# A graph attention layer: one head's mask added by VectorE, the residual in other buffers, and a new instruction scheduler

## The chip, the cores and the metric

The kernel runs on one core of one Trainium2 chip. The metric is the device time of one execution in microseconds (us); the median of several executions is quoted. All runs here were in the normal ("fast") state. A ratio is the recorded ratio of one kernel's fast runs to the kernel before's fast runs of the same rounds on the same chip. It is not quite the ratio of the medians quoted, nor that of the plain means (up to 0.2 points off; a point is 1% of the kernel before's time). Ratios are what is compared across rounds. The rounds of the experiments ran on five chips, and an interval covers its own rounds alone.

Engine names in the profile: PE is TensorE, PEld its weight load, DVE VectorE, ACT ScalarE, POOL GpSimd (which in both kernels' profiles issues the accumulating transfers alone, 428 and 368 of them, on the software queue) and SP the engine that issues all plain transfers and transposes there. SPq is SP's queue.

## The reference, cut to what matters

For 32 graphs of 512 nodes with 512 features: layer norm and relu, a graph attention layer with 4 heads of 256, elu, a second one with one head of 512, and a residual.

```
def gat_layer(x, mask, W, a_src, a_dst, bias, concat):
    xl = (x @ W).reshape(B, N, H, F)
    e = leaky_relu(asrc[:, :, None, :] + adst[:, None, :, :], 0.2)
    e = where(mask[..., None], e, -1e9)
    attn = softmax(e, axis=1)
    out = einsum('bsdh,bshf->bdhf', attn, xl)
    ...
mask = (adj > 0) | eye(N)          # adj of the inputs is symmetric
h = elu(gat_layer(h, mask, W1, ..., b1, concat=True))
x + gat_layer(h, mask, W2, ..., b2, concat=False)
```

## The kernel before

The program first records every operation as a job (engine, assumed cost, what it reads and writes); a list scheduler then orders each engine's queue, and only that order is emitted. The waits come from the data, so an order can be slow but not wrong. A job's `cost` and `size` are the scheduler's beliefs and reach the chip only through the order.

The products are done in seven block products instead of eight (Strassen's scheme), so VectorE forms sums of blocks before and after each product. All graphs are pipelined: while one graph's second layer runs, the next one's first layer and the one after's projection run beside it.

The mask `m` (0 or a large negative number, bf16, one buffer for all graphs) is built by VectorE. It is stored to DRAM as `md` (in the profile: dm) and transposed by a transfer into `mt`:

```
def masks(b):
    ...                                        # m[:, t, :] from adj; m = max(m, diag)
    if b < B - 1:
        MASK[b] = mk, md = mds.take()
        dma(512e3, every, [mk], md..., m...)
    tk, mt = mts.take()
    prog.add("SP", 2.2, every, [tk],
        lambda: nc.sync.dma_start_transpose(mt..., m...), 300e3)
```

`first(h)` makes the row scores of a head with `mt`; `second(h)` makes the attention itself, p, and adds the mask either on VectorE from `m` or by two transfers that accumulate `md` into p:

```
here = self.b == B - 1 or self.layer == 1 and (h in HERE or self.b == 0 and h < H - 1)
for u in range(NT):
    dve(..., scalar_tensor_tensor, p[:, u, :], ...)
    if here:
        dve(..., nc.vector.tensor_add, p[:, u, :], p[:, u, :], m[:, u, :])
if not here:
    for us in (0, 1), (2, 3):
        accumulate(500e3, keys + [mk], keys, p..., md...)     # a GpSimd transfer with accum_op=add
```

The residual, x plus the second bias, waits in four buffers until the last products are added to it:

```
def residual(b, places=(xrs,) * NT):
    for d in range(NT):
        xk, xr = places[d].take()
        dma(256e3, (), halves, xr, x[b, d * P : (d + 1) * P, :])
        if places[0] is xrs:
            accumulate(256e3, [xk], halves, xr, rows_of(b2, P))
        else:
            dve(..., nc.vector.tensor_add, xr, xr, b2_sb)
```

The elu uses the same `xrs` (xr) buffers. The first gather, `sums1`, uses `ts_` (t), also four, for its sums of p. One round of the main loop:

```
gather1(s, 0); s.second(2); s.second(3)          # s: first layer of graph i+1
S2[i] = second_layer(i); S2[i].second(0)         # second layer of graph i
masks(i + 2); project1(i + 2) ...; n.first(0) ...  # front of graph i+2
gather1(s, 1)
residual(i); gather2(i, ...)
load(i + 3); project2(i + 1, ...)
```

## Time and profile before

| | kernel before |
|---|---|
| time, median (range) | 2859.48 us (2850.74 to 2864.9) |
| span in the profile | 2856.2 us |
| TensorE busy / idle | 2774.1 / 82.1 us |
| VectorE busy | 2584.4 us (90%) |
| accumulating transfers: mask into p, bias into xr | 304 and 124 |
| software queue: bytes, share of the time of the 16 transfer engines | 191.92 MB, 30.3% |

Idle time of an engine is span less busy time. TensorE bounds the kernel; what it waits for is in the prediction. Two views also belong here. The page's list of transfers gives the size and the median time from issue to landing for those of GpSimd:

```profile
p<-dm POOLq DMA_DIRECT2D x304, 512.0 KB, 5.1
...
xr<-in_L_gnn_b_dram POOLq DMA_DIRECT2D x124, 256.0 KB, 5.8
```

And the view of the mask tile m, for the transpose (count, then least, median and greatest duration of the issue in ns). SP issued nothing else meanwhile in the stretches shown here:

```profile
L463 SPq DMA_TRANSPOSE mt<-m x32: 1572/1923/4054, 32.2 to 2697.4; - x32
```

In the timeline around one of these transposes, the neighbours on GpSimd's queue are 14 us before it and 9 us behind it. SP goes on 0.05 us after its end:

```profile
1557.41 0.86 POOL L327 DMA_DIRECT2D p<-dm  x1 [2.94 <-PE mm L333]
1580.67 0.86 POOL L327 DMA_DIRECT2D p<-dm  x1 [22.40 <-DVE p L319]
```
```profile
1571.34 1.58 SPq L463 DMA_TRANSPOSE mt<-m  x1
1572.97 1.30 SPq L322 DMA_DIRECT2D rr<-drr  x1
```

### The profile page before, as it was taken

The page shows a single profiled execution, that of the slowest core. Times are in us where ns is not written, and L with a number is a line of the kernel's source. Part 1 is how long each engine was busy: PE and PEld are TensorE (multiplying, and loading weights), DVE is VectorE, ACT ScalarE, POOL GpSimd, SP SyncE. Part 2 cuts the span into 40 slices and gives each one's busy share as a digit, 9 for nine tenths or more (in the row PEclk, how much of TensorE's full clock was granted, in tenths as well). Part 3 has the DMA queues.
Part 4 walks back from the last instruction along what each step waited for, and adds up shares of the span by engine and source line. Part 5 has one row for each costly group of instructions (what it writes and reads, how often), then busy time and mean ns, then how long its engine had stood idle before and what let it go on. Part 6 is the DMA issues. An engine that isn't in the chain of part 4 may idle for free. (4 is left out here: it accounts for less than half of the span.)

```text
span 2856.2 us, 41534 instructions
## 1 busy us (share of the span) xinstructions
PE 2774.1 (97%) x12456; PEld 2365.5 (83%) x12456; DVE 2584.4 (90%) x6567; ACT 2306.4 (81%) x4861; POOL 416.7 (15%) x466
## 2 busy tenths in 40 slices
PE   7999999999999999999999999999999999999997
PEld 6668888888888888888888888888888888888875
DVE  7979998989999989899898999999998999999995
ACT  6878798888888888887888888888888888888872
POOL 0011111111111111111111111111111111111100
PEclk9999999999999999999999999999999999999999
DMA  6577777687786777776777877778767778777724
GB/s 204 150 174 182 188 203 188 180 193 194 181 210 181 194 185 191 201 191 182 189 188 182 207 176 183 202 190 206 190 179 194 189 187 215 176 192 191 182 68 128
DMA packets 389455, 527.23 MB, mean 185 GB/s; under 512 B 227184, under 2 KB 231280, under 8 KB 389232
## 3 DMA queue, kind: packets, MB, share of 16 engines
q1 hardware_dynamic: 327600, 332.68, 41.7%
q0 software_dynamic: 61632, 191.92, 30.3%
q8 instruction: 99, 1.62, 0.2%
q14 instruction: 124, 1.02, 0.1%
HBM read 344.72 MB, written 50.79 MB: 138 GB/s over the span
## 5 line engine op out<-in xcount | busy, mean ns | idle before, releaser
L333 PE MATMUL mm<-w_sb,hs 128*128 128x257 f32 (+1 forms) x3024 | 693.2, 383 | 19.4 <-ACT xl L316 10.8
L333 PEld LDWEIGHTS mm<-w_sb,hs 128*128 128x128 f32 x3024 | 574.0, 191 | 113.6 <-ACT xl L316 20.0
L327 POOL DMA_DIRECT2D p<-dm x304 | 267.5, 882 | 2032.1 <-DVE p L319 1034.3
L316 ACT ACTIVATE l<-as,z 128x512 f32<-128x512 f32 x640 | 441.8, 723 | 113.6 <-DMA as<-das 101.7
L316 ACT ACTIVATE l<-l,low 128x512 f32<-128x512 f32 x640 | 459.5, 723 | 71.5 <-DVE low L319 69.0
L316 ACT ACTIVATE p<-p,z 128x512 f32<-128x512 f32 x640 | 432.8, 722 | 103.4 <-DMA p<-dm 75.2
L333 PE MATMUL mm<-p,xl 128*128 128x256 f32 (+1 forms) x2016 | 489.5, 391 | 6.4 <-ACT p L316 3.5
L319 DVE SCALAR_TENSOR_TENSOR p<-rr,z 128x512 f32<-128x512 f32 x640 | 457.8, 745 | 37.2 <-DMA rr<-drr 36.8
L333 PE MATMUL mm<-w_sb,ht 128*128 128x258 f32 x2112 | 481.5, 382 | 2.2 <-ACT xl L316 1.2
L333 PE MATMUL mm<-w_sb,h 128*128 128x257 f32 x2056 | 470.0, 380 | 6.2 <-DVE h L319 4.3
L319 DVE CUSTOM_DVE_ANT_1 l<-l,mt 128x512 f32<-128x512 f32 x640 | 427.4, 683 | 46.2 <-ACT l L316 44.8
L333 PEld LDWEIGHTS mm<-w_sb,ht 128*128 128x128 f32 x2112 | 400.5, 190 | 64.1 <-ACT xl L316 4.0
L333 PEld LDWEIGHTS mm<-p,xl 128*128 128x128 f32 x2016 | 382.9, 190 | 82.6 <-issue 19.4
L333 PEld LDWEIGHTS mm<-w_sb,h 128*128 128x128 f32 x2056 | 389.9, 190 | 65.7 <-DVE h L319 5.3
L316 ACT ACTIVATE xl<-mm 128x258 f32<-128x258 f32 (+2 forms) x752 | 281.7, 384 | 49.0 <-PE mm L333 46.5
L319 DVE TENSOR_TENSOR xl<-xl,mm 128x258 f32<-128x258 f32 x558 | 224.8, 417 | 36.6 <-PE mm L333 28.7
L316 ACT ACTIVATE h<-mm 128x256 f32<-128x256 f32 x480 | 175.4, 379 | 84.2 <-PE mm L333 82.0
L316 ACT ACTIVATE xr<-h,b_sb 128x512 f32<-128x512 f32 x240 | 171.5, 723 | 77.3 <-DVE h L319 76.8
L333 PE MATMUL mm<-t,hs 128*128 128x256 f32 x960 | 218.3, 380 | 1.2 <-ACT h L316 0.9
L333 PEld LDWEIGHTS mm<-t,hs 128*128 128x128 f32 x960 | 183.1, 191 | 27.0 <-ACT h L316 1.3
L319 DVE TENSOR_TENSOR xr<-mm,xr 128x256 f32<-128x256 f32 (+1 forms) x424 | 170.9, 417 | 28.4 <-PE mm L333 19.9
L319 DVE SCALAR_TENSOR_TENSOR h<-h,b_sb,xr 128x512 f32<-128x512 f32 x240 | 175.9, 745 | 20.0 <-ACT xr L316 19.2
(105 smaller groups left out, 3427.6 us busy)
## 6 DMA issues: line engine op xcount, KB each, us to landing
p<-dm POOLq DMA_DIRECT2D x304, 512.0 KB, 5.1
rr<-drr SPq DMA_DIRECT2D x160, 512.0 KB
x<-in_x_dram SPq DMA_DIRECT2D x129, 256.0 KB
adj<-in_adj_dram SPq DMA_DIRECT2D x128, 256.0 KB
as<-das SPq DMA_DIRECT2D x64, 512.0 KB
xr<-in_x_dram SPq DMA_DIRECT2D x124, 256.0 KB
xr<-in_L_gnn_b_dram POOLq DMA_DIRECT2D x124, 256.0 KB, 5.8
out_dram<-xr SPq DMA_DIRECT2D x124, 256.0 KB
```

Source lines behind the costliest of these rows:

```text
L316: prog.add("ACT", cost, reads, writes, lambda: nc.scalar.activation(*a, **k))
L319: prog.add("DVE", cost, reads, writes, lambda: f(*a, **k))
L327: lambda: nc.gpsimd.dma_start(to, at, accum_op=OP.add), 1.4 * size,
L333: f(*a, **k)
```

## The change

Three parts. (H) The fourth head's mask in the first layer is added by VectorE, which takes 60 accumulating transfers away. (T) The residual moves from the xr to the t buffers, so that it can be loaded before the elu is done. (S) The scheduler gets costs closer to measured ones, decides transfers no earlier than 3.5 us ahead, and runs 40 more passes that raise the rank of what stood in the chain before a gap of TensorE. The diff, cut to its core (most changed costs are left out):

```
-    CROSS, SAME = 0.15, 0.1
-    DMA_LEAD, DMA_TAIL, DMA_RATE = 1.2, 1.0, 280e3
+    CROSS, SAME = 0.15, 0.07
+    PAIRS = {("PE", "ACT"): 0.21, ("PE", "DVE"): 0.21, ("DVE", "POOL"): 0.58, ("POOL", "DVE"): 0.4}
+    DMA_LEAD, DMA_TAIL, AHEAD = 0.8, 2.0, 3.5
...
+    def sooner(self, rank, start, cause):
+        jobs, lost, free = self.jobs, {}, 0.0
+        for j in range(len(jobs)):
+            if jobs[j][0] != "PE":
+                continue
+            gap, free = start[j] - free, start[j] + jobs[j][1]
+            d = cause[j]
+            while gap > 0.05 and d is not None and start[j] - start[d] < self.SPAN:
+                lost[d] = max(lost.get(d, 0.0), gap)
+                d = cause[d]
+        return [r - self.GAIN * lost.get(j, 0.0) for j, r in enumerate(rank)]
...
+            if e in ("SP", "POOL"):
+                t = max(t, hold)
...
+        for _ in range(self.REPAIRS):
+            rank = self.sooner(rank, start, cause)
+            start, cause = look(rank)
...
-    HERE = ()
+    HERE = (3,)
...
-            here = self.b == B - 1 or self.layer == 1 and (h in HERE or self.b == 0 and h < H - 1)
+            here = self.b == B - 1 or self.layer == 1 and (h in HERE if self.b else h < H - 1)
...
-                        500e3, keys + [mk], keys,
+                        2.2, keys + [mk], keys,
...
-    def residual(b, places=(xrs,) * NT):
+    def residual(b, places=(ts_,) * NT):
...
-            if places[0] is xrs:
-                accumulate(256e3, [xk], halves, xr, rows_of(b2, P))
+            if places[0] is ts_:
+                accumulate(1.56, [xk], halves, xr, rows_of(b2, P))
```

More of the change, by code (lines that the diff above doesn't have):

```diff
@@ L78, in latency @@
         if self.jobs[a][0] != self.jobs[b][0]:
-            return self.CROSS
+            return self.PAIRS.get((self.jobs[a][0], self.jobs[b][0]), self.CROSS)
         return 0.0 if self.jobs[a][0] == "PE" else self.SAME
@@ L85, in forwards @@
         n = len(jobs)
+        cause = [None] * n
         left = [len(job[2]) for job in jobs]
@@ L94, in forwards @@
         while len(done) < n:
-            j, t = self.next_job(rank, free, soon, ready, tensor, left, ready_at)
+            j, t = self.next_job(rank, free, soon, ready, tensor, left, ready_at, landed - self.AHEAD)
             start[j] = t
@@ L99, in forwards @@
             if jobs[j][4] is not None:
-                landed = max(landed, t + jobs[j][1] + self.DMA_LEAD) + jobs[j][4] / self.DMA_RATE
+                landed = max(landed, t + jobs[j][1] + self.DMA_LEAD) + jobs[j][4]
             for s in after[j]:
@@ L105, in forwards @@
                     r = t + jobs[j][1] + self.latency(j, s)
-                ready_at[s] = max(ready_at[s], r)
+                if r > ready_at[s]:
+                    ready_at[s], cause[s] = r, j
                 left[s] -= 1
@@ L109, in forwards @@
                     heappush(soon[jobs[s][0]], (ready_at[s], s))
-        return start, done
+        return start, done, cause
+    def sooner(self, rank, start, cause):
[9 more added lines that the diff above has]
+        return [r - self.GAIN * lost.get(j, 0.0) for j, r in enumerate(rank)]
+    SPAN, GAIN = 60.0, 2.0
     def backwards(self, rank):
@@ L124, in backwards @@
                 if jobs[j][4] is not None:
-                    moving = max(moving, ready_at[j]) + jobs[j][4] / self.DMA_RATE
+                    moving = max(moving, ready_at[j]) + jobs[j][4]
                     ready_at[j] = moving + self.DMA_LEAD
@@ L141, in backwards, with next_job @@
                     found.append(d)
-    def next_job(self, rank, free, soon, ready, tensor, left, ready_at):
+    def next_job(self, rank, free, soon, ready, tensor, left, ready_at, hold=0.0):
         best = None
@@ L178, in order @@
         for j in reversed(range(n)):
-            later = self.DMA_LEAD + self.DMA_TAIL + (jobs[j][4] or 0.0) / self.DMA_RATE
+            later = self.DMA_LEAD + self.DMA_TAIL + (jobs[j][4] or 0.0)
             need[j] = max(
@@ L190, in order, with look @@
                 pe = j
-        rank, best, self.tried = need, None, []
-        for _ in range(self.ROUNDS):
-            back = self.backwards(rank)
-            late = [-back[j] - jobs[j][1] for j in range(n)]
-            start, done = self.forwards(late)
+        best, self.tried = None, []
+        def look(rank):
+            nonlocal best
+            start, done, cause = self.forwards(rank)
             end = max(start[j] + jobs[j][1] for j in range(n))
@@ L198, in order @@
             if best is None or end < best[0]:
-                best = end, start, done, late
-            rank = [-start[j] - jobs[j][1] for j in range(n)]
-        _, self.start, done, self.late = best
+                best = end, start, done, cause, rank
+            return start, cause
+        rank = need
+        for _ in range(self.ROUNDS):
+            back = self.backwards(rank)
+            rank = [-back[j] - jobs[j][1] for j in range(n)]
+            start, cause = look(rank)
+            rank = [-start[j] - jobs[j][1] for j in range(n)]
+        _, start, _, cause, rank = best
+        for _ in range(self.REPAIRS):
+            rank = self.sooner(rank, start, cause)
+            start, cause = look(rank)
+        _, self.start, done, _, self.late = best
         return done
+    REPAIRS = 40
     def emit(self):
@@ L326, in accumulate @@
             "POOL", cost, reads, writes,
-            lambda: nc.gpsimd.dma_start(to, at, accum_op=OP.add), 1.4 * size,
+            lambda: nc.gpsimd.dma_start(to, at, accum_op=OP.add), size,
         )
@@ L360, in weights1 @@
                     dma(
-                        256e3, (), [("w1", ix, k)], w1_sb[:, ix, k, :, 2:],
+                        0.75, (), [("w1", ix, k)], w1_sb[:, ix, k, :, 2:],
                         w1[row : row + P, :].rearrange("p (j c f) -> p c j f", j=H // 2, c=2)[:, c],
@@ L370, in scores1 @@
                 dma(
-                    256e3, (), [vk + ("v", a, j)], bc[:, 2 * a + j, :],
+                    0.75, (), [vk + ("v", a, j)], bc[:, 2 * a + j, :],
                     bass.AP(tensor=v.tensor, offset=v.offset + j * 2 * FH, ap=[[0, P], [1, 2 * FH]]),
@@ L397, in weights2 @@
             dma(
-                512e3, [("ht", 0, 0)], [("w2", ix)], w2_sb[:, ix, :, 1 - c : W2H - c],
+                1.5, [("ht", 0, 0)], [("w2", ix)], w2_sb[:, ix, :, 1 - c : W2H - c],
                 w2[r * HF // 2 : (r + 1) * HF // 2, c * DO // 2 : (c + 1) * DO // 2].rearrange(
@@ L402, in weights2 @@
             )
-        dma(4e3, (), ["b1"], b1_sb[:, 0], b1.rearrange("(c p) -> p c", p=P))
+        dma(0.1, (), ["b1"], b1_sb[:, 0], b1.rearrange("(c p) -> p c", p=P))
         dve(TINY, ["b1"], ["b1"], nc.vector.tensor_scalar_mul, b1_sb[:, 1], b1_sb[:, 0], -1.0)
-        dma(256e3, (), ["b2"], b2_sb, rows_of(b2, P))
+        dma(0.75, (), ["b2"], b2_sb, rows_of(b2, P))
         for a, v in enumerate((as2, ad2)):
             lk, bc = ls.take()
-            dma(256e3, (), [lk], bc, rows_of(v[0], P))
+            dma(0.75, (), [lk], bc, rows_of(v[0], P))
             for (r, c), ix in AT.items():
@@ L437, in load @@
             xk, xt = xs.take()
-            dma(256e3, (), [xk], xt, x[b, t * P : (t + 1) * P, :])
+            dma(0.75, (), [xk], xt, x[b, t * P : (t + 1) * P, :])
             XT[b].append((xk, xt))
@@ L444, in masks @@
             ak, a = adjs.take()
-            dma(256e3, (), [ak], a, adj[b, t * P : (t + 1) * P, :])
+            dma(0.75, (), [ak], a, adj[b, t * P : (t + 1) * P, :])
             dve(
@@ L458, in masks @@
             MASK[b] = mk, md = mds.take()
-            dma(512e3, every, [mk], md.rearrange("p t n -> p (t n)"), m.rearrange("p t n -> p (t n)"))
+            dma(0.45, every, [mk], md.rearrange("p t n -> p (t n)"), m.rearrange("p t n -> p (t n)"))
         tk, mt = mts.take()
@@ L465, in masks @@
             ),
-            300e3,
+            2.5,
         )
@@ L494, in norm_turn @@
         act(
-            0.62, [xk, sk + (t,)], [xk], hn, hn, AF.Relu,
+            0.71, [xk, sk + (t,)], [xk], hn, hn, AF.Relu,
             bias=st[:, t, S : S + 1], scale=st[:, t, S + A : S + A + 1],
@@ L514, in norm_turn @@
             act(
-                1.14, [xk], [ak], words.rearrange("p (h f) -> p h f", h=2),
+                0.96, [xk], [ak], words.rearrange("p (h f) -> p h f", h=2),
                 hn.bitcast(U16).rearrange("p (f h) -> p h f", h=2), AF.Copy,
@@ L523, in norm_turn @@
                 ),
-                200e3,
+                1.27,
             )
             act(
-                1.14, [xk], [("ht", t, 0), ("ht", t, 1)],
+                1.21, [xk], [("ht", t, 0), ("ht", t, 1)],
                 ht[:, :, t * P : (t + 1) * P].bitcast(U16).rearrange("p k (n h) -> p h k n", h=2),
@@ L563, in spread @@
             dma(
-                0, [ok], [dk], dr[:k].rearrange("k (b j) -> b k j", j=32),
+                0.03, [ok], [dk], dr[:k].rearrange("k (b j) -> b k j", j=32),
                 bass.AP(
@@ L570, in spread @@
             dma(
-                256e3 * rows, [dk], [ok], o[:, :rows].rearrange("p r n -> p (r n)"),
+                0.72 * rows, [dk], [ok], o[:, :rows].rearrange("p r n -> p (r n)"),
                 bass.AP(tensor=dr.tensor, offset=dr.offset, ap=[[0, P], [1, rows * N]]),
@@ L746, in sevens @@
             pe(
-                akeys + rkeys(n), [bk], kh * width / 597,
+                akeys + rkeys(n), [bk], kh * width / 593,
                 [
@@ L808, in project1_first @@
                            for q in (("w1", AT[r, c], k), ("w1s", AT[r, c], k, j))],
-                        [bk], KT * 0.435,
+                        [bk], KT * 0.437,
                         [
@@ L839, in scores_1, with elu @@
         return [zk + (0,)]
-    def elu(g, places, at, cost):
+    def elu(g, places, at):
         keys = [("h1", g, r) for r in range(2)]
         ek, e = xrs.take()
-        act(cost, [*places, "b1"], [ek], e, at, AF.Exp, bias=b1_sb[:, 0, g : g + 1], scale=-1.0)
+        act(0.62, [*places, "b1"], [ek], e, at, AF.Exp, bias=b1_sb[:, 0, g : g + 1], scale=-1.0)
         act(0.54, [ek], [ek], e, e, AF.Relu, bias=1.0, scale=-1.0)
@@ L868, in gather1_plain @@
                     )
-                elu(h * FPH + f, [bk], ps, 0.6)
+                elu(h * FPH + f, [bk], ps)
                 banks.give(bk)
@@ L937, in gather1 @@
             pe(
-                akeys + wkeys, [bk], KQ * M / 597,
+                akeys + wkeys, [bk], KQ * M / 593,
                 [
@@ L957, in gather1 @@
             if n in (3, 4):
-                elu(g, [("h1", g, q) for q in range(2)], h1[:, g, :], 0.54)
+                elu(g, [("h1", g, q) for q in range(2)], h1[:, g, :])
         for i in range(2):
@@ L1021, in residual @@
             halves = [xk, xk + (0,), xk + (1,)]
-            dma(256e3, (), halves, xr, x[b, d * P : (d + 1) * P, :])
-            if places[0] is xrs:
-                accumulate(256e3, [xk], halves, xr, rows_of(b2, P))
+            dma(0.75, (), halves, xr, x[b, d * P : (d + 1) * P, :])
+            if places[0] is ts_:
+                accumulate(1.56, [xk], halves, xr, rows_of(b2, P))
             else:
@@ L1069, in put @@
                 upper[u[0]] = -1
-                dma(256e3, [xk, xk + (0,), xk + (1,)], (), out[b, d * P : (d + 1) * P, :], xt)
+                dma(0.75, [xk, xk + (0,), xk + (1,)], (), out[b, d * P : (d + 1) * P, :], xt)
                 place.give(xk)
@@ L1094, in gather2_plain @@
             dve(0.6, [bk, xk], [xk], nc.vector.tensor_add, xr, ps, xr)
-            dma(256e3, [xk], (), out[b, d * P : (d + 1) * P, :], xr)
+            dma(0.75, [xk], (), out[b, d * P : (d + 1) * P, :], xr)
             banks.give(bk)
```

## The prediction

> **What bounds the kernel now.** I began with the page's list of busy times, then the costliest groups, then the waits of TensorE alone, then busy times by stretch, and last the timeline around single gaps.
>
> ```profile
> span 2856.2 us, 41534 instructions
> PE 2774.1 (97%) x12456; PEld 2365.5 (83%) x12456; DVE 2584.4 (90%) x6567; ACT 2306.4 (81%) x4861; POOL 416.7 (15%) x466
> ```
>
> TensorE is busy for 97% of the span, so the prize can hardly be more than the 2856.2 - 2774.1 = 82.1 us in which it stands idle, plus what it loses inside its busy time. To split that up I take three stretches (columns: start:end and length, then busy us and instruction count of PE, PEld, DVE, ACT and POOL, then the granted clock, DMA share and GB/s).
>
> ```profile
> 0.00:200.00 200.00, 172.44 (x629) 123.49 (x630) 152.75 (x470) 147.30 (x300) 18.07 (x25) 0.96 0.68 173
> 200.00:2700.00 2500.00, 2463.33 (x11257) 2131.79 (x11256) 2311.36 (x5831) 2079.82 (x4385) 388.20 (x429) 1.00 0.75 191
> 2700.00:2856.20 156.20, 138.30 (x574) 110.17 (x572) 120.27 (x268) 79.31 (x176) 10.42 (x12) 0.95 0.37 98
> ```
>
> Idle TensorE time is 27.6 us in the start, 36.7 us in the middle and 17.9 us in the end. An undisturbed stream shows the pace: 16 matmul records of 256 columns take 3.62 us with the last one's 0.38 us of latency in it, so (3.62 - 0.38) / 15 = 0.216 us a record. In the middle 11257 records at about 0.2167 us (257 columns on average) are 2439 us; some 70 of them are 512 wide and cost another 15 us. So of the middle's 2500 us about 2454 us are needed and about 46 us are lost: 36.7 us idle and 9 us of drained tails and slow clock. By the same sum the start loses about 51 us and the end about 25 us. The total floor is near 2730 us.
>
> What TensorE waits for in the middle stretch (us in total, times, longest):
>
> ```profile
> PE mm L333 <- DVE hs L319: 13.1, 5, 3.6
> PE mm L333 <- DVE xr L319: 11.8, 17, 2.3
> PE mm L333 <- ACT xl L316: 5.7, 12, 0.9
> PE mm L333 <- ACT h L316: 5.0, 6, 1.8
> ```
>
> These two named first are what the change aims at. One xr case in the timeline, where I traced the wait to its source:
>
> ```profile
> 1504.26 0.86 POOL L327 DMA_DIRECT2D xr<-in_L_gnn_b_dram  x1 [4.53 <-DMA xr<-in_x_dram]
> ...
> 1506.65 0.86 POOL L327 DMA_DIRECT2D xr<-in_L_gnn_b_dram  x1 [1.53 <-DMA xr<-in_x_dram]
> ...
> 1511.40 1.09 DVE L319 TENSOR_TENSOR xr<-mm,xr 128x256 f32<-128x256 f32 x3 [1.84 <-DMA xr<-in_L_gnn_b_dram]
> 1511.88 1.13 PE L333 MATMUL mm<-xl,hs 128*128 128x256 f32 x4 [1.15 <-DVE xr L319]
> ```
>
> The last gather of a graph adds its products into a residual (x plus the bias). That residual sits in the four xr buffers, which the elu of the gather before also needs. So the load of x comes late, the bias is accumulated into it only 2 to 7 us before the data is needed, VectorE waits for the landing and TensorE for VectorE to empty a PSUM bank. The hs waits have another cause: at 2204.5 us TensorE stood for 2.72 us because VectorE's first sum of the second layer's p waited for ScalarE's exponential, which its queue held behind another head's work. That is the order of the queues, not the length of an operation.
>
> [...] the existing mask adds have a median of 685 ns here[...]. [...] the 5 us from 1680 us, with a 3.0 us gap, were granted 0.85. [...] here the software queue takes 30.3% of them, with 191.92 MB.
>
> **The change part by part.**
>
> *Fourth head's mask.* For graphs 1 to 30 head 3 of the first layer no longer gets its mask by two accumulating DMAs; VectorE adds it in four adds of 128x512. Removed: 30 x 2 = 60 of 304 p<-dm transfers, 60 x 0.88 = 53 us of GpSimd, which is idle anyway, and 60 x 0.524 = 31.5 MB, so about 5% of the span of DMA engine time. Added: 120 adds; the group p<-p,m in the list by shape has 32 in 20.9 us, so 0.653 us each, 78 us of VectorE busy time. None of it is on TensorE's path by itself. But about 71 us fall in the middle, where VectorE has 2500 - 2311 = 189 us idle: that leaves 118 us, and about 95 us once the span shrinks, so VectorE would stand at 96%. The gain is one landing of 5.1 us (median) less before head 3's exponentials; ScalarE waits 75.2 us in total for such landings, but ScalarE has 500 us to spare. By itself I count this as -3 us by shorter chains and +6 us by a tighter VectorE: +3 us.
>
> *Residual in the t buffers.* Those are taken by the first gather's sums of p and come free at its products 5 and 6, six of 14 product steps before its end; a step is 4 records, 0.86 us. Six steps (5.2 us), then 14 steps of the projection (12.2 us) pass before the last gather begins: 17 us, for a load of x plus an accumulate of 5.8 us. Before, only the 12 us after the gather less the elu's tail were left. So nearly all xr waits should go: 11.8 us idle plus, by the weight loads' waits for xr (25.7 us in all against TensorE's 12.8), as much again hidden in tails. I take -13 us. The elus also get all four xr buffers at all times: ScalarE and VectorE waits on each other there (76.8 and 31.2 us) shrink, which does not show directly.
>
> *Schedule mended.* The queue orders come from a list scheduler in the program. Its durations and latencies are made closer to what was measured (593 columns per us in place of 597, the ScalarE costs, the DMA model), DMA issues are no longer decided far ahead, and 40 more passes raise the rank of whatever stood in the chain before a TensorE gap and keep the best order. This is aimed at hs, xl and h waits: 13.1 + 5.7 + 5.0 = 24 us in the middle, plus about 3 us of slow clock behind the long ones. Half of what remains of a model's gaps is my choice, as the model cannot see the true DMA landings: -13 us. In the start and end the gaps are mostly chains without other work to put in (first input, last softmax): -2 us.
>
> Sum: +3 - 13 - 13 - 2 = -25 us. From the median of 2859.5 us: 2834 us.
>
> **The rivals.** First, VectorE becomes the bound. For: 96% in the middle, and each added 0.65 us sits in a strict queue before sums that TensorE needs. Against: its gaps are short waits, 40 us for ScalarE's l and 31 us for rr landings, that other work may fill. If it won, the gain would be eaten: 2855 to 2880 us. Second, the t buffers become the new wait. The next graph's t sums started at 1536 us in the stretch above, and two of the outputs left xr only at 1533.9 us; with the residual in t, those sums must wait for the output's landing. The scheduler can issue it earlier, as the gather had ended by 1518.2 us. If it fails, 1 to 2 us in each of 30 graphs come back: 2850 to 2870 us. Third, the mask tile m must now live until head 3's adds, so the next graph's masks start later. In the trace the m writes begin at 1560.0 us, already behind the p work of about 1556 us, so I expect at most 3 us from it. Fourth, the repair works far better than half: all 46 us of the middle and a few of the start vanish, 2805 to 2812 us.
>
> **Range and chances.** Two per cent faster is 2802 us, which needs 57 us, more than the whole middle loses; I give it 0.05. Two per cent slower is 2917 us, which needs VectorE to stall TensorE 2 us in every graph; 0.03. The range from 2810 us (nearly all middle gaps gone) to 2856 us (gains eaten by VectorE or by t) should hold it 8 times in 10. Within 2%: 0.92.
>
> **What would show it right or wrong.** VectorE busy up by about 78 us with p<-p,m at 152 instructions; p<-dm at 244; software queue near 160 MB. TensorE's waits for xr in the middle below 3 us shows the buffer step right. The hs, xl and h waits near 12 us show the repair's half; near 0 or still 24 us show it mis-sized. New TensorE or VectorE waits behind t with the output's landing as their releaser would show the second rival; a rise in waits for hs, h and xl from VectorE with its idle time under 80 us the first. TensorE's busy time should stay within 10 us of 2774 us, with its idle time near 57 us; if the time moves otherwise, my floor is wrong.

## The result, and the profile after

The changed kernel takes 2960.79 us (median of 4, 2936.76 to 2974.6) against 2856.45 us: ratio 1.0354 (95% interval 1.028 to 1.0428). It is slower, where I had foreseen a gain of 25 us. (With one run more, the median of the kernel before is 2856.45 us here and 2859.48 us above.)

```profile
span 2954.9 us, 41539 instructions
## 1 busy us (share of the span) xinstructions
PE 2799.3 (95%) x12456; PEld 2376.6 (80%) x12456; DVE 2640.2 (89%) x6687; ACT 2311.9 (78%) x4861; POOL 373.8 (13%) x406
```

TensorE does the same 12456 matmul records. It is idle for 2954.9 - 2799.3 = 155.6 us in place of 82.1 us, and busy 25 us longer (its mean granted clock, the share of full speed that it was allowed, fell from 0.992 to 0.979). VectorE has grown by 55.8 us only, not 78 us, and its share has fallen from 90% to 89%. The same stretches as before, the middle now 2600 us long:

```profile
0.00:200.00 200.00, 174.40 (x648) 124.45 (x649) 158.42 (x484) 148.95 (x300) 16.32 (x23) 0.97 0.62 171
200.00:2800.00 2600.00, 2488.03 (x11244) 2143.69 (x11243) 2359.62 (x5926) 2082.96 (x4386) 347.02 (x371) 0.98 0.74 172
```

The start is no worse. The loss is in the middle: TensorE idles 112 us there, against 36.7 us, and VectorE idles too, 240 us. So no other engine has become the bound; all of them wait. What TensorE waits for in the middle:

```profile
PE mm L368 <- DVE t L354: 38.5, 23, 6.5
PE mm L368 <- ACT p L351: 32.7, 14, 13.0
PE mm L368 <- DVE xl L354: 19.4, 1, 19.4
PE mm L368 <- DVE hs L354: 13.2, 2, 11.4
```

The residual's waits, now called t, have not gone but tripled (11.8 to 38.5 us), and single waits of 11 to 19 us are new. I followed the longest back in the timeline, on POOL, SP, DVE and PE:

```profile
2145.40 0.86 POOL L362 DMA_DIRECT2D t<-in_L_gnn_b_dram  x1 [20.04 <-DVE m L354]
2145.94 1.21 POOL L362 DMA_DIRECT2D p<-dm  x1
2148.15 0.86 POOL L362 DMA_DIRECT2D p<-dm  x1 [1.00 <-DVE p L354]
2148.69 3.00 POOL L362 DMA_DIRECT2D t<-in_L_gnn_b_dram  x3
```
```profile
2145.90 12.50 SPq L498 DMA_TRANSPOSE mt<-m  x1
2158.53 2.18 SPq L357 DMA_DIRECT2D dm<-m  x1
...
2175.98 0.69 DVE L354 CUSTOM_DVE_ANT_1 l<-l,mt 128x512 f32<-128x512 f32 x1 [21.70 <-DMA mt<-m]
...
2179.09 3.81 PE L368 MATMUL mm<-w_sb,ht 128*128 128x258 f32 x8 [19.43 <-DVE xl L354]
```

Six accumulating transfers, four of the bias and two of a mask, are issued within 4 us of the start of the mask's transpose. Its issue takes 12.5 us, VectorE can use it only 30 us after it began, and VectorE and then TensorE stand still for it. The transfer engines were not idle meanwhile; in these 10 us their busy share is above 1 while little moves (last two columns: share and GB/s; the whole span's mean before was 185 GB/s):

```profile
2160.00:2165.00 5.00, 0.00 (x0) 0.00 (x0) 0.00 (x0) 0.00 (x0) 0.00 (x0) 0.91 1.20 125
2165.00:2170.00 5.00, 0.00 (x0) 0.00 (x0) 0.00 (x0) 0.00 (x0) 0.00 (x0) 0.50 1.43 116
```

This graph has the longest wait, but the meeting is the rule:

```profile
L498 SPq DMA_TRANSPOSE mt<-m x32: 1539/10142/14654, 33.6 to 2798.4; - x32
```
```profile
p<-dm POOLq DMA_DIRECT2D x244, 512.0 KB, 6.3
...
t<-in_L_gnn_b_dram POOLq DMA_DIRECT2D x124, 256.0 KB, 10.3
```

The median transpose takes 10.1 us of SP's time in place of 1.9 us, and the bias lands after 10.3 us in place of 5.8 us. I counted in the timeline of GpSimd, for the 28 graphs of the middle, the accumulating transfers issued from 8 us before a mask transpose until the end of its issue. Before: none, but for one that was issued 0.2 us before the end of one transpose. After: six in all of them but one, which has five.

VectorE's own waits show both late landings, that of the mask tile and that of the bias. In the kernel before it had no such wait for mt, and 7.8 us in all for the bias:

```profile
DVE l L354 <- DMA mt<-m: 39.9, 9, 21.7
...
DVE t L354 <- DMA t<-in_L_gnn_b_dram: 14.0, 6, 7.3
```

### The profile page after: what moved, and what is told of

It reads as the page before. It is cut to its first block, busy times and chain, and to the rows that moved or that the text cites. A ratio compares the mean times of both kernels' runs of the same rounds, so it can differ in the third digit from the quotient of the medians.

```text
span 2954.9 us, 41539 instructions
## 1 busy us (share of the span) xinstructions
PE 2799.3 (95%) x12456; PEld 2376.6 (80%) x12456; DVE 2640.2 (89%) x6687; ACT 2311.9 (78%) x4861; POOL 373.8 (13%) x406
## 3 DMA queue, kind: packets, MB, share of 16 engines
q0 software_dynamic: 52992, 160.46, 26.2%
## 5 line engine op out<-in xcount | busy, mean ns | idle before, releaser
L368 PE MATMUL mm<-p,xl 128*128 128x256 f32 (+1 forms) x2016 | 503.1, 396 | 41.1 <-ACT p L351 40.3
L351 ACT ACTIVATE p<-p,z 128x512 f32<-128x512 f32 x640 | 430.6, 717 | 98.7 <-DMA p<-dm 61.8
L354 DVE CUSTOM_DVE_ANT_1 l<-l,mt 128x512 f32<-128x512 f32 x640 | 425.9, 682 | 50.1 <-DMA mt<-m 39.9
L362 POOL DMA_DIRECT2D p<-dm x244 | 219.8, 908 | 1531.3 <-PE mm L368 581.5
L354 DVE TENSOR_TENSOR t<-mm,t 128x256 f32<-128x256 f32 (+1 forms) x424 | 169.3, 416 | 37.8 <-PE mm L368 23.5
L368 PE MATMUL mm<-xl,p 128*128 128x256 f32 (+1 forms) x752 | 185.4, 396 | 6.9 <-ACT p L351 6.7
## 6 DMA issues: line engine op xcount, KB each, us to landing
t<-in_L_gnn_b_dram POOLq DMA_DIRECT2D x124, 256.0 KB, 10.3
```

What stands on the lines that cost most here:

```text
L351: prog.add("ACT", cost, reads, writes, lambda: nc.scalar.activation(*a, **k))
L354: prog.add("DVE", cost, reads, writes, lambda: f(*a, **k))
L362: lambda: nc.gpsimd.dma_start(to, at, accum_op=OP.add), size,
L368: f(*a, **k)
```

## The experiments

Four theories. **A**: accumulating transfers that run beside the mask's transpose slow it, and the chain behind it stalls TensorE. **B**: the new scheduler is worse on the chip by itself. **C**: VectorE's 78 us of mask adds are the cost. **D**: the residual holds the t buffers, which the next sums of p then wait for. "Near" in the table is the median, over the 28 middle graphs, of the GpSimd transfers counted as above (for the plain copies of e13 to e15, which issue in 0.53 us, within 8 us to either side).

| run | parts | ratio (95%) | median us | transpose issue, median us | near |
|---|---|---|---|---|---|
| changed kernel | H T S | 1.0354 (1.028 to 1.0428) | 2960.79 | 10.1 | 6 |
| e1 | S | 1.0195 (1.0173 to 1.0217) | 2911.68 | 1.9 | 0 |
| e2 | T S | 0.9959 (0.9944 to 0.9974) | 2845.82 | 2.6 | 0 |
| e3 | H S | 1.0323 (1.0301 to 1.0345) | 2948.19 | 4.5 | 4 |
| e4 | H T | 1.0616 (1.0592 to 1.064) | 3034.48 | 7.7 | 6 |
| e5 | H T S, no bias transfer | 1.0116 (1.0068 to 1.0164) | 2897.43 | 6.2 | 2 |
| e6 | H T S, bias a plain copy | 1.0151 (1.0083 to 1.022) | 2912.7 | 7.2 | 6 (4 plain) |
| e7 | H T S, residual behind | 1.0056 (1.0036 to 1.0075) | 2881.9 | 2.0 | 0 |
| e8 | T S, residual behind | 1.001 (0.9989 to 1.0031) | 2870.99 | 1.9 | 0 |
| e9 | H | 1.005 (1.0032 to 1.0069) | 2878.95 | 3.0 | 0 |
| e10 | T | 1.0086 (1.006 to 1.0111) | 2888.63 | 1.9 | 0 |
| e11 | T S, extra VectorE work | 1.0189 (1.016 to 1.0218) | 2917.9 | 2.9 | 0 |
| e12 | T S, chosen by collisions | 1.0016 (0.9996 to 1.0036) | 2870.42 | 1.9 | 0 |
| e13 | H T S, plain mask copy | 1.0095 (1.0071 to 1.0118) | 2892.9 | (0.53) | 6 |
| e14 | H T, plain mask copy | 0.9936 (0.9911 to 0.9961) | 2846.53 | (0.53) | 6 |
| e15 | none, plain mask copy | 0.9977 (0.9961 to 0.9994) | 2856.65 | (0.53) | 0 |
| e16 | H T, residual behind | 0.995 (0.9931 to 0.9968) | 2848.22 | 1.9 | 0 |

By the verdicts on record, at 2%, the changed kernel, e3 and e4 are slower, e1, e6 and e11 unclear, and all others the same as the kernel before. Smaller differences rest on the intervals.

Times against the expectations: e5, e6, e8 and e13 were 3 to 13 us slower than the ranges that theory A gave, and e14 was 13 us faster; the other misses are told below.

### e1 to e4: the parts apart and in pairs

e1 is the changed kernel with both other parts undone:

```
-    HERE = (3,)
+    HERE = ()
-    def residual(b, places=(ts_,) * NT):
+    def residual(b, places=(xrs,) * NT):
-            if places[0] is ts_:
+            if places[0] is xrs:
```

> Only the new scheduler; mask of the fourth head by DMA and the residual in the xr buffers, as before. In the plan the scheduler makes, 0 to 2 accumulating DMAs lie near a mask transpose. Theory A (accumulating DMAs that run beside the transpose of the next mask slow it from about 2 us to 10 us of issue, and the chain behind it stalls TensorE): transposes stay near 2 us and the time is 2830 to 2880 us. Theory B (the new scheduler itself is worse on the chip): slower than 2900 us with transposes near 2 us. Theory C (VectorE's 78 us of mask adds): not in here, so about 2855 us.

The transposes stay at 1.9 us with nothing near, and the kernel is 2% slower all the same. Theory A's time was missed; theory B has something in it: the new scheduler's orders can be worse on the chip. TensorE's waits of the whole run show where: on the residual, which still sits in xr.

```profile
PE mm L368 <- DVE xr L354: 51.3, 43, 4.6
```

e2 undoes only the mask adds (the first two lines of the diff above).

> The changed kernel with the fourth head's mask by DMA again: new scheduler, residual in the t buffers. The plan has about 2 accumulating DMAs near each mask transpose, unevenly (0 to 5). Theory A: transposes between 2 and 6 us on average, time 2860 to 2910 us, between the two kernels. Theory B: about 2955 us still. Theory C: back to about 2850 us, whatever the transposes do. Theory D (residual in t makes the next sums of p wait): about 2955 us still.

It is faster than the kernel before, by 0.4%. Theory D falls here: the residual sits in t and does no harm. Theory A's time was too pessimistic, as the plan's accumulating transfers did not meet the transposes on the chip, except in 3 graphs, in which five or six did; there the issue took 11.4, 13.8 and 10.5 us, everywhere else in the middle 4.2 us or less.

e3 undoes only the residual's place (the last four lines of the diff of e1).

> The changed kernel with the residual in the xr buffers again: new scheduler, mask adds on VectorE. The plan has 5 to 6 accumulating DMAs near nearly every mask transpose. Theory A: transposes of 8 us or more and a time of 2930 us or more, although the residual is where it was. Theory D: about 2855 us. Theory C: about 2930 us with transposes of 2 us.

The time is as theory A said, the transposes are not: 4.5 us, not 8. Most of the loss is e1's wait on the residual, which has grown to 69.0 us. So e3 doesn't single out A.

e4 puts the mask adds and the t buffers into the kernel before, with its old scheduler:

```
-    HERE = ()
+    HERE = (3,)
-            ... (h in HERE or self.b == 0 and h < H - 1)
+            ... (h in HERE if self.b else h < H - 1)
-    def residual(b, places=(xrs,) * NT):
+    def residual(b, places=(ts_,) * NT):
-            if places[0] is xrs:
+            if places[0] is ts_:
```

> The kernel before with the mask adds and the residual in t, but with the old scheduler. The plan has 6 accumulating DMAs near every mask transpose. Theory A: transposes of 10 us or more, time 2940 us or more. Theory B: faster than 2870 us. Theories C and D: 2930 to 2960 us with transposes near 2 us.

This is the slowest of all, 6.2%. Six accumulating transfers stand at every transpose, and the residual keeps TensorE waiting:

```profile
PE mm L333 <- DVE t L319: 129.3, 40, 9.6
```

Theory B as the main cause falls: without the new scheduler it is worse, not better. VectorE itself waits 61.8 us for the bias to land and 39.4 us for the mask tile.

### e5 to e8: the same places, other transfers

e5 keeps every queue's order and drops only the bias transfers. The scheduler still believes in the job; nothing is emitted for it.

```
-                accumulate(1.56, [xk], halves, xr, rows_of(b2, P))
+                prog.add("POOL", 0.95, [xk], halves, lambda: None, 1.56)
```

> The changed kernel with every instruction where it is, but the 124 accumulating transfers of the bias into the residual are not issued (the result is wrong on purpose: no second bias). VectorE, ScalarE, TensorE and the queues of plain transfers have the same order. Theory A (accumulating transfers beside the mask transpose): the transposes fall from 10 us to 3 to 6 us, as two mask accumulations are still near each, and the time falls to 2830 to 2890 us. Theory C (VectorE's load) and theory D (residual holds the t buffers): the time stays at 2930 us or more, since the adds and the holding of t are the same.

The result is wrong on purpose (relative error 0.04). The ratio falls from 1.0354 to 1.0116, with the same VectorE work, so C and D do not hold these 2.4 points. The two mask accumulations that remain keep the transpose at 6.2 us.

e6 issues the bias as a plain copy: same queue, same bytes, same places, no addition.

```
-                accumulate(1.56, [xk], halves, xr, rows_of(b2, P))
+                prog.add("POOL", 0.95, [xk], halves,
+                    lambda xr=xr: nc.gpsimd.dma_start(xr, rows_of(b2, P)), 1.56)
```

> The changed kernel with every instruction where it is, but the same 124 transfers of the bias are plain copies, of the same size, from the same GpSimd queue at the same places, without the addition (wrong on purpose: the bias overwrites x). If it is the accumulation[...] that does not go with the transpose: transposes of 3 to 6 us and 2830 to 2900 us, as without the transfers. If any transfer from that queue does it: transposes near 10 us and about 2957 us.

Also wrong on purpose (0.82). More than half of the loss is gone, 1.0151, although the transpose's issue is still at 7.2 us. In the same places the bias landed after a median of 8.8 us copied, against 10.3 us accumulated in the changed kernel. So the accumulation carries more of it than the transfer (2.0 points go without the addition, 2.4 without the transfer in e5), and the issue time alone is not a measure of the loss.

e7 lets the residual's load of x follow the transpose on SP, so that the accumulation comes after both. Unlike e5 and e6 it makes the scheduler plan anew, so every queue's order can change:

```
+            late = [MASKT[b + 2][0]] if b + 2 < B and places[0] is ts_ else []
-            dma(0.75, (), halves, xr, x[b, d * P : (d + 1) * P, :])
+            dma(0.75, late, halves, xr, x[b, d * P : (d + 1) * P, :])
```

> The changed kernel, right result, with one more dependency for the scheduler: the load of x for the residual stands behind the transpose of the next mask but one in the transfer queue, so that its accumulation comes after it. Mask adds on VectorE and residual in t stay. The plan has 2 accumulating transfers near each transpose (mask accumulations). Theory A: transposes of 3 to 6 us and 2850 to 2900 us. Theory C: 2930 us or more. Theory D: 2930 us or more.

```profile
L498 SPq DMA_TRANSPOSE mt<-m x32: 1557/1962/6882, 33.2 to 2719.7; - x32
```

All three parts are in, VectorE has all its adds, and the ratio is 1.0056. Here the mask accumulations have moved away from the transposes too, which the plan did not foresee: they mostly start 4 to 8 us after the transpose. Theories C and D as main causes fall; what is left above 1 is 0.6 points.

e8 is e7 with `HERE = ()`.

> The same dependency with the fourth head's mask by DMA again. The plan has about one accumulating transfer near a transpose. Theory A: transposes of 2 to 4 us and 2825 to 2860 us, near the 2846 us of the kernel without mask adds. Theory C: about the same. This one is also a candidate for beating both kernels.

It gives 1.001, within noise of the kernel before, and 0.5 points under e7, which is a first size for the mask adds without a collision. As a candidate it is no better than e2.

### e9 to e12: single parts, VectorE's load, a candidate

e9 is the kernel before with the two H lines of e4's diff, e10 the one with its four T lines.

> The kernel before with the mask adds alone: old scheduler, residual in xr. The plan has 2 accumulating transfers near each mask transpose, because the transpose now follows the fourth head's adds and the same stretch holds the mask accumulations of the heads before. Theory A: transposes of 4 to 6 us and 2880 to 2940 us. Theory C (only VectorE's load of 78 us counts, which by the two kernels with the residual behind the transpose costs some 15 us): 2860 to 2880 us.

> The kernel before with the residual in t alone: old scheduler, fourth head's mask by DMA. The plan has about 2 accumulating transfers near a transpose, unevenly, up to 5. Theory A: transposes of 2 to 5 us, the time between 2850 and 2900 us, slower where more collide. If residual in t helps by itself, as my prediction says: 2845 us.

On the chip neither has an accumulating transfer near its transposes, unlike the plan. (In e9 two mask transfers mostly follow 3 to 8 us after the transpose's start, and its issue takes 3.0 us.) The time of e9 fell into theory C's range, and that of e10 into theory A's, though without A's collisions. Each part alone costs little, 0.5 and 0.9 points. Together they should then cost 1.4 points; e4 measured 6.2. That surplus of 4.8 points is what neither part has alone. e10 also shows my buffer step at work: TensorE's waits for xr were 12.8 us in all before, and no wait for t, where the residual now sits, stands in the list; the 1.0 us for xr falls in the first 200 us, before any residual. But the total did not fall, as waits for hs and p rose to 31.1 us each.

```profile
PE mm L333 <- ACT p L316: 31.1, 14, 8.5
PE mm L333 <- DVE hs L319: 31.1, 22, 4.0
...
PE mm L333 <- DVE xr L319: 1.0, 1, 1.0
```

e11 takes e2, keeps its order, and emits one more VectorE instruction of the same size behind each attention instruction of head 3 in graphs 1 to 30:

```
+                def twice(to, *a, more=self.layer == 1 and h == 3 and 0 < self.b < B - 1, **k):
+                    nc.vector.scalar_tensor_tensor(to, *a, **k)
+                    if more:
+                        nc.vector.tensor_max(to, to, to)
-                    ... keys, nc.vector.scalar_tensor_tensor,
+                    ... keys, twice,
```

> The new scheduler with the residual in t and the fourth head's mask by DMA, which took 2846 us, in the same order of every engine, with one more 128x512 VectorE instruction (a maximum of p with itself, so the result is right) behind each of the 120 that the mask adds would follow; the scheduler doesn't know of them. That is VectorE's load of the change without its effect on where the mask transpose stands. Theory C: 2900 us or more. Theory A: 2850 to 2880 us, with the transposes as in that run.

It costs 1.0189 - 0.9959 = 2.3 points, some 66 us for about 74 us of added busy time. That is theory C's number. So VectorE's time is dear when the order doesn't count on it: TensorE's waits for `ACT xl` grew from 19.1 to 48.5 us. But the mask adds of the change are known to the scheduler, and then they cost 0.5 points (e7 against e8; e9 against the kernel before). I also built the opposite, the changed kernel without its adds; it passed no check and was not run, and this left no record.

e12 lets the scheduler choose among its orders with a price on collisions:

```
             end = max(start[j] + jobs[j][1] for j in range(n))
+            turns = [start[j] for j in range(n) if jobs[j][:2] == ("SP", 2.2)]
+            end += 1.5 * sum(-6 < start[j] - t < 5
+                for j in range(n) if jobs[j][0] == "POOL" and jobs[j][4] is not None for t in turns[3:31])
```

> A candidate: new scheduler, residual in t, fourth head's mask by DMA; when it keeps the best of its 52 orders, the scheduler adds 1.5 us for every accumulating transfer planned from 6 us before to 5 us after a mask transpose. The order kept has 4 such transfers where the best before had 14, and no graph with more than 2. Theory A: no transpose over 8 us in the middle, and 2825 to 2845 us, faster than both kernels and than the 2846 us of the run without this. If the collisions of 3 graphs cost nothing: 2846 us or slower.

No transpose in the middle is over 3.2 us, as wanted, and the time is no better than before: 1.0016. Taking the collisions of 3 graphs away brought nothing; as the whole order changed with them, what they alone cost is not shown. This was a miss.

### e13 to e16: the transpose itself

Until here the burst of six accumulating transfers could have been slow by itself. The adjacency of these inputs is symmetric, so the transposed mask can also be read from an untransposed copy. e13 keeps all queues as they are and makes each mask transpose a plain copy of the same 512 KB:

```
-            lambda: nc.sync.dma_start_transpose(
-                mt.rearrange("p t d r -> p (t d) r"), m.rearrange("p t n -> p (t n)")
+            lambda: nc.sync.dma_start(
+                mt.rearrange("p t d r -> p (t d r)"), m.rearrange("p t n -> p (t n)")
...
-                    out=e3, in0=e3, in1=mt[:, :, d, :], scale=-1.0, ...
+                    out=e3, in0=e3, in1=mt[:, d, :, :], scale=-1.0, ...
```

> The changed kernel with every instruction of every queue where it is, but each transpose of the mask is a plain copy of the same 512 KB (the adjacency of these inputs is symmetric, so reading the copied tile in the other order gives the right result here; for other inputs it would not). The six accumulating transfers stay. If accumulation and transpose together are the cause: 2860 to 2890 us, near the 1.0056 of the kernel with the residual behind the transpose, and no wait of TensorE over 5 us in the middle for the residual. If the burst of accumulating transfers is slow by itself: 2940 us or more, and the bias still lands after 10 us.

```profile
L498 SPq DMA_DIRECT2D mt<-m x32: 520/531/777, 33.4 to 2735.7; - x32
```
```profile
p<-dm POOLq DMA_DIRECT2D x244, 512.0 KB, 6.4
t<-in_L_gnn_b_dram POOLq DMA_DIRECT2D x124, 256.0 KB, 10.5
```

The result is right, 1.0095 in place of 1.0354. The bias still lands after a median of 10.5 us, so the burst alone is slow in that sense, and for the residual it does little: TensorE's waits for t fall from 38.5 to 9.0 us, and VectorE's for the bias and the mask tile to 0.5 and 1.0 us. TensorE's waits for ScalarE's p rise, though, from 47.5 to 62.9 us (17.0 us in e7); whether the burst or the order makes them is not shown. What goes away with the transpose is the tail (the longest bias landing is 14.1 us, against 31.4 us) and the blocked SP queue (0.53 us of issue, against 10.1 us). Which of these two carried the loss, the runs do not separate.

e14 makes the same exchange in e4.

> The same exchange in the kernel before with mask adds and residual in t under the old scheduler, which took 1.0616 of the time of before. If the pair is the cause: 2860 to 2920 us. If the burst alone is: 3000 us or more.

From 1.0616 to 0.9936: one operation exchanged 32 times takes 6.8 points, 195 us, away, and the slowest kernel of the study becomes the fastest by ratio. The bias still lands after a median of 10.4 us (10.8 us in e4), yet TensorE's waits for t, 129.3 us in e4, are nearly gone:

```profile
PE mm L333 <- DVE t L319: 7.5, 12, 1.5
```

It relies on symmetric inputs, so it is a proof and not a version to keep.

e15 is the control, the exchange in the kernel before.

> Control: the kernel before, every instruction where it is, with each mask transpose a plain copy of the same bytes. Its transposes had no accumulating transfer near. If only the pair costs: within 0.5% of the kernel before (2850 to 2875 us). If a plain copy in place of a transpose is a gain anywhere: faster than 0.99.

0.9977: where nothing accumulates beside the transpose, a plain copy gains 0.2 points. So the gains of e13 and e14 are not the copy's own; the pair costs about 2.6 - 0.2 = 2.4 points in the changed kernel and 6.8 - 0.2 = 6.6 in e4. The exchange is not complete: the 124 other transposes (x<-adj, 256 KB) stay, and ScalarE waits for them 52.1 us in e13 and 39.3 us in e14, against 11.5 us before. They too issue more slowly in company: counted in the changed kernel's trace, a median of 1.25 us with no GpSimd transfer in flight and 3.4 us with four.

e16 keeps both parts and the true transpose, under the old scheduler, with the load of x behind the transpose (e7's edit on e4).

> A candidate with the right result for any input: the kernel before with mask adds and residual in t under the old scheduler, and the load of x for the residual behind the mask transpose in the transfer queue. If keeping the bias accumulations away from the transpose is what matters: 2840 to 2890 us instead of 1.0616 of the time of before; below 2850 us only if the mask accumulations stay away too.

```profile
L463 SPq DMA_TRANSPOSE mt<-m x32: 1548/1936/4266, 37.8 to 2703.9; - x32
```

0.995, right for any input: one added dependency, with the order that the scheduler then makes, is worth 6.7 points here, and the version beats both kernels. By ratio it is as good as e2; the gain is a quarter of what counts as faster at 2%, but its interval (0.9931 to 0.9968) lies clear of 1. In its middle VectorE is busy for 94.7% of the time, and TensorE does not stall on it:

```profile
200.00:2700.00 2500.00, 2465.73 (x11267) 2128.98 (x11266) 2368.71 (x5929) 2079.29 (x4382) 345.27 (x371) 1.00 0.70 178
```

## Why the prediction was wrong

It said 2834 us, with a range up to 2856 us and a chance of 0.03 for two per cent slower; it was 2961 us.

**Where the time goes.** The counts came as foretold (152 mask adds, 244 mask transfers, 160.46 MB on the software queue), and TensorE stayed the bound. The loss is waiting in the middle and TensorE's 25 us of longer busy time, for which the prediction allowed 10 us. One reading was wrong: of the 512-column records that it puts in the middle, some 70, the trace has none there (128 in the start, 32 in the end). By its own sum the middle then lost about 61 us and the start about 36 us, not 46 and 51; the total stays.

**Fourth head's mask, +3 us.** Mis-sized, not wrong in kind. With the scheduler informed and no collision it cost 0.5 points, 13 us (e7 against e8, e9). VectorE did not become the bound, at 94.7% in e16. The first rival is right about the danger: as much work, unknown to the schedule, cost 66 us (e11).

**Residual in the t buffers, -13 us.** The waits for the residual can vanish where the landing is undisturbed (none in e10, 0.6 us in e8), though 7 to 12 us stay in e2, e16 and e7. In the changed kernel they grew to 38.5 us. The step that failed is "17 us, for a load of x plus an accumulate of 5.8 us": it took the landing time of the trace before as a property of the transfer. It had been measured where these transfers stood apart from the mask transposes. In the changed kernel the median landing took 10.3 us, which 17 us may still hold and which is no better without the transpose (10.5 us in e13); but the longest took 31.4 us, against 14.1 us in e13. The tail beside the transpose broke the step.

**Mask tile m lives longer, "at most 3 us from it".** This is the other half of the failed step. I asked when the transpose would start, not what would stand beside it. The mask adds hold m, so the next mask's transpose falls behind the attention work of heads 2 and 3 and beside the mask transfers of that stretch; the t buffers let the bias transfers come early, into the same microseconds. Each alone keeps clear (e9, e10), both together collide in every graph (e4). (The places are read from the traces; the reasons for them only from the program.) I had priced two changes to the transfer traffic one by one, as if they shared nothing.

**Schedule mended, -13 - 2 us.** This step failed too, and its sign depends on the rest. The new scheduler alone costs 2.0 points (e1). There the waits at which it aimed (hs, xl and h in the middle, 24 us before, foretold near 12) fell to 16.7 us, but those for xr rose from 11.8 to 51.3 us: the waiting moved to the residual. With H and T and no collision it is still dearer than the old one: e7 over e16 by 1.1 points, e13 over e14 by 1.6. With T alone it helps: e2 under e10 by 1.3. With the collision it helps, 1.0354 against 1.0616, because it meets it less badly. That its costs are closer to measured ones did not make its order better on the chip. The scheduler prices an accumulating transfer and a transpose the same wherever they stand, so its search has no reason to keep them apart; this is argued from its code, and e12 shows only that it can be made to.

**The sum.** Of the 3.5 points, the pair of accumulating transfers and transpose holds about 2.4 (e13, less e15's share) to 3.0 (e7). The rest, 0.6 to 1.1 points, goes with the new order; under the old one the same parts give 0.995 (e16). Since e7's order is another one, its 3.0 is not the pair's alone.

**The second rival** named the right place (waits for t) and the wrong reason: the next sums of p waited for an output's landing for 2.4 us in total, once.

What stays open: why accumulation and transpose hinder each other, and how the loss divides between the blocked SP queue and the late landings. VectorE's waits (39.9 us for the mask tile, 14.0 us for the bias) show that the late landings had a part.

## What to carry to other kernels

A transfer's time to land, read from a trace, belongs to the order it was read in: here the same bias of 256 KB took a median of 5.8 us before and 10.3 us after. Before a change that moves transfers, list for each moved one what it will run beside, above all accumulating transfers beside a transpose (the pair cost 2.4 points in the changed kernel and 6.6 in e4), and keep the two apart by a dependency, as e16 does (0.995, against 1.0616). And when parts of a change act on the same resource, run them alone and in pairs: here each alone cost under 1 point, and the two together over 6.
